# Moving two groups of matmuls in the block loop of a transformer layer: the gate's third pass and eight down products

## The chip, the cores and the metric

The kernel runs on one NeuronCore of one Trainium2 chip. TensorE (PE) multiplies into PSUM (8 banks of 128 x 512 float32 here); ScalarE (ACT), VectorE (DVE) and GpSimd (POOL) do the rest, of which GpSimd works on SBUF alone in this kernel; SyncE (SP) issues DMAs. Each engine takes its instructions in a fixed order and waits for others by semaphores. The metric is the device time of one execution in microseconds (us), as a median over runs.

## The reference: what is computed

8192 tokens (4 x 2048) of 256 features pass through one layer, post-norm, in float32:

```python
Q, K, V = x @ W_q.T, x @ W_k.T, x @ W_v.T
decay = sigmoid(log_decay[0])
mask = where(diff >= 0, decay ** diff, 0)        # 32 x 32, within a chunk of 32 tokens
S = einsum('bncd,bnkd->bnck', Qc, Kc) * mask     # scores, chunk by chunk
O = einsum('bnck,bnkd->bncd', S, Vc)
gate = sigmoid(x @ W_g.T)
attn = gate * O @ W_o.T + x
h = layernorm(x + attn)

g = h @ (w_gate / 127).T      # 768 hidden features, integer weights from -127 to 127
u = h @ (w_up / 127).T
out = layernorm(h + (silu(g) * u) @ (w_down / 127).T)
```

## The kernel before

The tokens are cut into 16 blocks of 512 (`TB`, `NB`). Everything is unrolled; a block's tensors lie either feature-major (features on partitions, 512 tokens along the row) or token-major (`NG` = 4 groups of 128 tokens).

**Parts.** To keep float32 accuracy on the fast matmul formats, operands are split in parts. An activation or weight of the attention becomes `hi`, `lo` and `gap` (`token_parts`, L464; `weight_parts`, L442): ScalarE makes `hi`, GpSimd makes `lo` = t - hi (L473), VectorE makes `gap` (L479, in a closure `gaps` that is called later). A product of two such operands is made by `three` (L526) in **three passes**: hi x hi and lo x lo go into a PSUM bank, ScalarE scales the bank in place (L533), then gap x gap is added (the third pass, in the closure `others`, L535) and `finish` reads the bank. Two banks are used per product. In the hidden layer `hT` and `u` are split in `hi` and an fp16 `lo` (L887/L888, L936/L937), the integer weights are stored in both types, and each product is hi x hi plus lo x lo.

**The loop.** Iteration `b` of L1141 (0 to 13) runs the hidden layer of block b, and beside it the attention of later blocks: `n = b + 2` is in its output projection, `m = b + 3` in its projections of y (the query and key matrices folded in one), value and gate. The hidden layer's 768 features come in six chunks of 128 (`ffn_up`, L900: fg and fu on PE, silu on ScalarE, the product u on VectorE, then the split: u_hi on ScalarE, u_lo on GpSimd). For b from 1 to 12 the order of PE's work, written out by hand, is:

1. chunks 0 and 1, the first two passes of y of block m, chunk 2, the third pass of y;
2. chunk 3, the scores `ps` of block m (L654; they read `yT`, the copy of y by VectorE, L558), the products with the values (L690) of block n, chunk 4;
3. the first two passes of the value (`split_v`) and of the gate (`split_gate`), the value's third pass (`v_rest`, L1199), chunk 5 (L1202);
4. the first two passes of the output projection (`split_out`, L1208), the **gate's third pass** (`g_rest`, L1211), whose results ScalarE turns into tanh (L550), and the output projection's third pass (`out_rest`, L1212), after which VectorE adds the residual (L820) and takes the mean and variance of the rows (L338, L339);
5. the **down product** of block b (`ffn_down`, L954): for b > 2 by `project_back_late` (L746), 24 products of high parts (six chunks of 128 hidden features, four token groups each), then 24 of low parts, into two banks.

The end of the iteration on the other engines, in program order: ScalarE casts the transposed h of block b + 1 (`split_h`, L887) right after the output projection's scaling and before the gate's tanh; then it makes x_hi of the block after m (`token_parts`, L1217), the two square roots of the layer norms (L347, between two table loads), and, in the next iteration, normalizes h (L426). GpSimd makes hT_lo (L888) and x_lo (L473). VectorE takes the moments, then `between` (L1223): the reciprocal, three small operations `minus`, `scale` and `shift` (L386 to L389), and the gaps of x; then the residual of the down product (L971) with its moments, and then u of the next block's chunk 0 (L931).

**What sets the order.** Nearly every instruction is pinned by `in_turn` (L115), which keeps program order on its engine; the splits of h on GpSimd and the DMAs are not pinned. PSUM banks are taken in turn from a pool of 8 (`bank`, L118), so that the bank of a new product is the one whose user came eight requests ago; the two banks of the down product are requested after the two of the output projection. DMAs go by SP's queue: per block one load of x, one of xT, one store of the output, and 16 small ones that move the 32 x 32 transposed pieces of h (L870).

Of the kernel before, what the change touches and what calls it, by code (L numbers as in the profile page):

```python
# [59 lines left out]
NG = TB // P  # L60
# [16 lines left out]
def kernel(  # L77
# [665 lines left out]
                    in_turn(product)  # L743
            finish(slice(h * per, (h + 1) * per), pb)

    def project_back_late(b, parts, ws, finish, name, between):  # L746


        per = TB // D
        banks = [bank(f"{name}_{b}_{h}") for h in range(NG // per)]  # L750
        hi, lo = (list(zip(part, w)) for part, w in zip(parts, ws))

        def product(g, part, w, first=False):
            in_turn(
                nc.tensor.matmul(  # L755
                    banks[g // per][:, g % per * D : (g % per + 1) * D],
                    lhsT=part[:, g * P : (g + 1) * P],
                    rhs=w,
                    start=first and g % per == 0,
                    stop=True,  # L760
                    skip_group_check=True,
                )
            )

        for i, term in enumerate(hi):
            for g in range(NG):
                product(g, *term, first=i == 0)
        for h in range(NG // per):
            for term in lo:
                for g in range(h * per, (h + 1) * per):  # L770
                    product(g, *term)
        between()
        for h, pb in enumerate(banks):
            finish(slice(h * per, (h + 1) * per), pb)

    def chunked(t):
        return [t[:, k, :] for k in range(t.shape[1])]
# [173 lines left out]
        hi, lo = (list(zip(part, w)) for part, w in zip(parts, ws))  # L951
        return hi[:-2] + lo[:-2], hi[-2:] + lo[-2:]

    def ffn_down(b, uT, h, between=None, chunkwise=False, amid=None):  # L954


        r = work.tile([P, NG, D], F32, tag="r2", name=f"r2_{b}")
        mv = no_moments(f"f{b}")
        made = None
        order = in_turn  # L960
        late_residuals = not chunkwise and b > 2

        def begin():
            nonlocal made
            if between is not None:
                made = between()

        def residual(gs, pb):

            order(  # L970
                nc.vector.scalar_tensor_tensor(  # L971
                    flat(r, gs), pb, SCALE**2 / U_UP * H_UP, flat(h, gs), ALU.mult, ALU.add
                )
            )
            moments(r, f"f{b}", range(gs.start, gs.stop), order, mv)
            if not late_residuals and gs.start == 0:
                begin()

        ws = [chunked(w) for w in fd]
        if chunkwise:  # L980
            per = TB // D
            banks = [bank(f"fdn_{b}_{k}") for k in range(NG // per)]
            for late, terms in enumerate(early_and_late(uT, ws)):
                if late and amid is not None:
                    made = amid()
                for k, pb in enumerate(banks):
                    for i, (part, w) in enumerate(terms):
                        for j in range(per):
                            g = k * per + j
                            product = nc.tensor.matmul(  # L990
                                pb[:, j * D : (j + 1) * D],
                                lhsT=part[:, g * P : (g + 1) * P],
                                rhs=w,
                                start=late + i + j == 0,
                                stop=True,
                                skip_group_check=True,
                            )
                            in_turn(product)
                    if late:
                        residual(slice(k * per, (k + 1) * per), pb)  # L1000
        else:
            if late_residuals:
                project_back_late(b, uT, ws, residual, "fdn", begin)
            else:
                project_back(b, uT, ws, residual, "fdn")
        return r, mv, made
# [134 lines left out]
    for b in range(NB - 2):  # L1141
        n = b + 2
        m = b + 3
        more = m < NB
        xns[n] = load_xn(n)
        if b and m + 1 < NB:
            xTs[m + 1] = load_xT(m + 1)
        hT = hTs.pop(b)
        uT = ([], []) if b else uT_0
        sT, v, sg = ahead  # L1150
        if not more:
            scales_next = iterated_scale_and_shift(mv_out, of_out, f"out_{b}")
        if b:
            normalize(hs[b + 1], *scales_h)
            up_now(b, hT, uT, 0)
        multiply = ffn_up(b, hT, uT, range(1, 2), held=True)
        if b:
            moving = move_h(b + 1, hs[b + 1])
        else:
            cast_fd(0, range(2, 3))  # L1160
            multiply()
            x_gaps()
            sT = attn_scores(n, yT)
            xTs[m + 1] = load_xT(m + 1)
        if more:
            yT, y_rest = split_y(m, x_parts)
        if b:
            multiply()
        if not more:
            goT = attn_values(n, sT, v, sg)  # L1170
        multiply = ffn_up(b, hT, uT, range(2, 3), held=True)
        if b > 1:
            normalize(r_before, *scales_out, range(NG // 2))
        multiply()
        if more:
            y_rest()
        if b == 0:
            normalize(hs[b + 1], *scales_h)
            moving = move_h(b + 1, hs[b + 1])
        if not more:  # L1180
            go_parts, go_gaps = token_parts(goT, f"go_{n}")
        multiply = ffn_up(b, hT, uT, range(3, 4), held=True)
        if b > 1:
            normalize(r_before, *scales_out, range(NG // 2, NG))
        multiply()
        if b > 1:
            store(b - 2, r_before)
        if more:
            sT_next = attn_scores(m, yT)
            goT = attn_values(n, sT, v, sg)  # L1190
            multiply = ffn_up(b, hT, uT, range(4, 5), held=True, low_first=True)
            go_parts, go_gaps = token_parts(goT, f"go_{n}")
            if b == 0:
                cast_fd(1, range(1))
            multiply()
            go_gaps()
            v_next, v_rest = split_v(m, x_parts)
            sg_next, g_rest = split_gate(m, x_parts)
            v_rest()  # L1199
            if b == 0:  # L1200
                cast_fd(1, range(1, 2))
            up_with_cast(b, hT, uT, 5, 1, range(2, 3))  # L1202
        else:
            up_now(b, hT, uT, 4)
            go_gaps()
        r_before = r_out
        if more:
            hs[n], out_rest = split_out(n, go_parts)  # L1208
            if b:
                hTs[b + 1] = split_h(b + 1, moving)  # L1210
            g_rest()  # L1211
            mv_h = out_rest()  # L1212
            if b == 0:
                hTs[b + 1] = split_h(b + 1, moving)
            ahead = sT_next, v_next, sg_next
            if m + 1 < NB:
                x_parts, x_gaps = token_parts(xTs[m + 1], f"x_{m + 1}")  # L1217
            std_h = root_in_turn(mv_h, of_h, f"h_{b}")
            if b:
                mv_before, std_before = mv_out, root_in_turn(mv_out, of_out, f"out_{b}")  # L1220
            back_to_silu()

            def between():  # L1223
                scales = scale_and_shift(
                    mv_h, std_h, of_h, f"h_{b}", nc.vector, in_turn
                )
                if m + 1 < NB:
                    x_gaps()
                return scales

            r_out, mv_out, scales_h = ffn_down(b, uT, hs.pop(b), between)
            if b:
                scales_out = scale_and_shift(mv_before, std_before, of_out, f"out_{b}")
        else:
            multiply = ffn_up(b, hT, uT, range(5, KH), held=True)
            hs[n], out_rest = split_out(n, go_parts)
            multiply()
            hTs[b + 1] = split_h(b + 1, moving)
            scales_out = scales_next
            normalize(r_before, *scales_out)  # L1240
            store(b - 1, r_before)

            def amid():
                return iterated_scale_and_shift(out_rest(), (HALF, 1.0), f"h_{n}")

            r_out, mv_out, scales_h = ffn_down(
                b, uT, hs.pop(b), chunkwise=True, amid=amid
            )
            scales_out = iterated_scale_and_shift(mv_out, of_out, f"out_{b + 1}")
# [361 lines left out]
```

## Time and profile before

| | before |
|---|---|
| median of 3 runs | 487.5 us (487.4 to 488.54) |
| the profiled execution, its own time | 486.83 us |
| span, first to last instruction | 485.2 us |
| granted TensorE clock, mean | 0.997 |
| period of one iteration, start of chunk 0 to the next (blocks 4 to 11) | about 29.2 us |
| busy in the stretch 192.29 to 221.50 us (block 5): PE, PEld, ACT, DVE, POOL | 29.21, 23.52, 22.95, 21.20, 16.72 us |
| mean duration: p_g third pass (128 x 512), p_o third pass (128 x 256), fdn high (128 x 256) | 393, 283, 281 ns |

The time is that of the whole execution on the device, the span that from the first to the last instruction of the program. PEld is the loading of the stationary operand into TensorE, which overlaps the matmuls. A matmul's duration contains the time that its last columns take through the array, so that consecutive matmuls overlap in the table: the pace is read from start to start (24 high down products from 216.12 to 218.95 us, so 0.118 us each, though one is listed with 281 ns). In a timeline each line gives the start, the length of the group, the engine, the line of the code, what is written from what, the shapes and the count; in brackets stands how long the engine was idle before it and what ended that.

### The profile page before, as it was taken

Reading aid. Unit: us, or ns where it says so; the run is one execution under the profiler, and the core shown is the slowest. Engines: PE = TensorE matmul, PEld = TensorE weight load, DVE = VectorE, ACT = ScalarE, POOL = GpSimd, SP = SyncE. Lnnn points to the kernel's source line nnn. Section 1 sums busy time; section 2 is a strip of 40 time slices with the busy share of each in tenths; the row PEclk is TensorE's granted clock in tenths of the full one; section 3 lists DMA queues with packets and bytes.
Section 4 is the critical chain, followed back from the end, with each engine's and each line's share of the span. In section 5 each row is a group of like instructions: output and inputs, shape, how many; then the busy total and the mean of one; then the engine's idle time right before and its main releaser. Section 6 shows DMA issues by size and latency. Waiting matters only on the chain.

```text
span 485.2 us, 12289 instructions
## 1 busy us (share of the span) xinstructions
PE 479.0 (99%) x4760; PEld 381.1 (79%) x4760; DVE 344.0 (71%) x795; ACT 371.3 (77%) x699; POOL 281.3 (58%) x285
## 2 busy tenths in 40 slices
PE   9999999999999999999999999999999999999995
PEld 5787787887868778797887968878697887868685
DVE  4687958687575976858777585975858777577656
ACT  4878697597887788687787877788687787776845
POOL 3835665555736565474555735566464655657764
PEclk9999999999999999999999999999999999999998
DMA  8720411211403114131321403113131211103002
GB/s 258 261 93 4 134 46 47 80 47 41 135 24 108 44 44 134 28 105 50 88 82 36 141 18 115 45 50 125 26 107 50 83 45 32 59 20 112 34 15 84
DMA packets 43323, 36.99 MB, mean 76 GB/s; under 512 B 4864, under 2 KB 39168, under 8 KB 43264
## 3 DMA queue, kind: packets, MB, share of 16 engines
q1 hardware_dynamic: 42144, 35.28, 23.8%
q10 hardware_dynamic: 1120, 0.92, 0.6%
q8 instruction: 38, 0.62, 0.6%
q14 instruction: 21, 0.17, 0.1%
HBM read 20.45 MB, written 8.39 MB: 59 GB/s over the span
## 4 chain that ended last, share of the span: by engine, by line
PE 99%; DVE 0%; ACT 0%; issue 0%
PE fg L911 18%; PE fu L911 18%; PE fdn L755 11%; PE p_o L514 9%; PE p_v L514 9%; PE p_y L492 9%; PE p_g L492 9%; PE po L690 4%; PE fdn L736 3%; PE ps L654 2%; PE fdn L990 2%; PE fdn L1353 1%; PE pg L578 1%; PE pv L620 1%; PE pa L799 1%; PE py L599 1%
## 5 line engine op out<-in xcount | busy, mean ns | idle before, releaser
L937 POOL TENSOR_TENSOR u_lo<-u,u_hi 128x512 f16<-128x512 f32 (+1 forms) x98 | 129.4, 1326 | 84.4 <-ACT u_hi L936 78.7
L931 DVE SCALAR_TENSOR_TENSOR u<-fu,s 128x512 f32<-128x512 f32 (+1 forms) x98 | 66.1, 675 | 72.5 <-ACT s L920 71.7
L936 ACT CAST u_hi<-u 128x512 fp32r<-128x512 f32 (+1 forms) x98 | 59.4, 606 | 45.7 <-DVE u L931 45.7
L920 ACT ACTIVATE s<-fg 128x512 f32<-128x512 f32 (+1 forms) x98 | 57.4, 585 | 41.5 <-PE fg L911 41.5
L911 PE MATMUL fg<-hT_hi,fg_hi 128*128 128x512 f32 (+1 forms) x196 | 72.8, 453 | 0.0
L911 PE MATMUL fu<-hT_hi,fu_hi 128*128 128x512 f32 (+1 forms) x196 | 60.3, 389 | 0.0
L911 PE MATMUL fg<-hT_lo,fg_lo 128*128 128x512 f16 (+1 forms) x196 | 58.2, 379 | 0.0
L911 PE MATMUL fu<-hT_lo,fu_lo 128*128 128x512 f16 (+1 forms) x196 | 57.4, 375 | 0.0
L473 POOL TENSOR_TENSOR go_lo<-goT,go_hi 128x512 fp32r<-128x512 f32 x30 | 44.6, 1510 | 18.2 <-ACT go_hi L472 18.2
L479 DVE SCALAR_TENSOR_TENSOR go_gap<-go_hi,goT 128x512 fp32r<-128x512 f32 x30 | 48.2, 1645 | 0.8 <-ACT go_hi L472 0.7
L473 POOL TENSOR_TENSOR x_lo<-xT,x_hi 128x512 fp32r<-128x512 f32 x30 | 37.7, 1277 | 14.1 <-ACT x_hi L472 14.1
L911 PEld LDWEIGHTS fg<-hT_hi,fg_hi 128*128 128x128 f32 x196 | 35.6, 190 | 10.3
L911 PEld LDWEIGHTS fu<-hT_hi,fu_hi 128*128 128x128 f32 x196 | 36.5, 188 | 8.1
L820 DVE TENSOR_TENSOR h<-p_o,x 128x512 f32<-128x512 f32 x30 | 19.3, 685 | 32.0 <-PE p_o L514 28.2
L888 POOL TENSOR_TENSOR hT_lo<-hT,hT_hi 128x512 f16<-128x512 f32 x28 | 35.7, 1296 | 4.0 <-ACT hT_hi L887 3.6
L911 PEld LDWEIGHTS <-fu_lo 128*128 128x128 f16 x196 | 19.2, 98 | 22.2
L388 POOL TENSOR_SCALAR minus_out<-rstd_out 128x4 f32<-128x4 f32 x12 | 2.6, 221 | 54.1 <-DVE rstd_out L386 54.1
L755 PE MATMUL fdn<-fd_hi,u_hi 128*128 128x256 f32 x240 | 29.9, 281 | 0.0
L755 PEld LDWEIGHTS fdn<-fd_hi,u_hi 128*128 128x128 f32 x240 | 29.0, 189 | 0.0
L911 PEld LDWEIGHTS <-fg_lo 128*128 128x128 f16 x196 | 13.1, 98 | 19.1 <-issue 12.9
L755 PE MATMUL fdn<-fd_lo,u_lo 128*128 128x256 f16 x240 | 27.9, 273 | 0.0
L426 ACT ACTIVATE h<-h,shift_h,scale_h 128x256 f32<-128x256 f32 x52 | 26.9, 587 | 0.7 <-DVE shift_h L389 0.7
(179 smaller groups left out, 1097.8 us busy)
## 6 DMA issues: line engine op xcount, KB each, us to landing
x<-in_x_dram SPq DMA_DIRECT2D x16, 512.0 KB, 3.8
xT<-in_xT_dram SPq DMA_DIRECT2D x15, 512.0 KB, 4.2
hT<-sq SPq DMA_DIRECT2D x224, 32.0 KB, 1.9
out_dram<-r SPq DMA_DIRECT2D x13, 512.0 KB, 3.2
out_dram<-r SPq DMA_DIRECT2D x7, 128.0 KB, 1.7
fg_int<-in_ffn_gT_dram SPq DMA_DIRECT2D x3, 256.0 KB, 7.4
fu_int<-in_ffn_uT_dram SPq DMA_DIRECT2D x3, 256.0 KB, 6.4
fd_int<-in_ffn_dT_dram SPq DMA_DIRECT2D x3, 256.0 KB, 5.5
```

What stands on the lines that cost most here:

```text
L426: nc.scalar.activation(r[:, g, :], r[:, g, :], AF.Identity, bias=shift[:, g : g + 1], scale=scale[:, g : g + 1],)
L473: in_turn(nc.gpsimd.tensor_tensor(lo[:, k, :], t[:, k, :], whole, ALU.subtract))
L479: nc.vector.scalar_tensor_tensor(gap[:, k, :], whole, -WHOLE, t[:, k, :], ALU.mult, ALU.add)
L492: nc.tensor.matmul(pb, lhsT=a[kind][:, k, i * P : (i + 1) * P], rhs=b[kind][:, k, :], start=kind + k == 0, stop=True, skip_group_check=True,)
L514: nc.tensor.matmul(pb[:, j * D : (j + 1) * D], lhsT=b[kind][:, k, g * P : (g + 1) * P], rhs=a[kind][:, k, :], start=kind + k + j == 0, sto ...
L755: nc.tensor.matmul(banks[g // per][:, g % per * D : (g % per + 1) * D], lhsT=part[:, g * P : (g + 1) * P], rhs=w, start=first and g % per ...
L888: nc.gpsimd.tensor_tensor(in_order[1], whole, in_order[0].bitcast(F32), ALU.subtract)
L911: product = nc.tensor.matmul(pb, lhsT=w[kind][:, dc, hc * P : (hc + 1) * P], rhs=hT[kind][:, dc, cols], start=(kind == kinds[0] and dc == ...
L920: in_turn(nc.scalar.activation(s, pg, AF.Silu, scale=SCALE / H_UP))
L931: nc.vector.scalar_tensor_tensor(u, pu, U_UP / H_UP, s, ALU.mult, ALU.mult)
L936: in_steady_turn(nc.scalar.copy(hi, u))
L937: in_steady_turn(nc.gpsimd.tensor_tensor(lo, u, hi.bitcast(F32), ALU.subtract))
```

## The change

In iterations with b > 2 that still prepare a later block (b = 3 to 12), two groups of matmuls take another place in PE's order:

- The gate's third pass (`g_rest`: 4 matmuls on PE and 2 tanh on ScalarE) is called directly after the value's third pass, ahead of chunk 5, and no longer between the output projection's first two passes and its third.
- `project_back_late` no longer runs the down product as a whole; it requests the banks and returns two functions, `high(chunks)` and `low()`. The first eight high products (chunks 0 and 1, four token groups each) are issued between the output projection's first two passes and its third; the other 16 and the 24 low ones follow the third pass as before, by `ffn_down`, which gets them in `begun`.

The small operations of `between`, the gaps and the residuals keep their order behind the low products. In iterations 0 to 2 and 13 and in the last two blocks the code does what it did.

```diff
-    def project_back_late(b, parts, ws, finish, name, between):
+    def project_back_late(b, parts, ws, name):
...
-        for i, term in enumerate(hi):
-            for g in range(NG):
-                product(g, *term, first=i == 0)
-        for h in range(NG // per):
-            for term in lo:
-                for g in range(h * per, (h + 1) * per):
-                    product(g, *term)
-        between()
-        for h, pb in enumerate(banks):
-            finish(slice(h * per, (h + 1) * per), pb)
+        def high(chunks):
+            for i in chunks:
+                for g in range(NG):
+                    product(g, *hi[i], first=i == 0)
+
+        def low():
+            for h in range(NG // per):
+                for term in lo:
+                    for g in range(h * per, (h + 1) * per):
+                        product(g, *term)
+            return [(slice(h * per, (h + 1) * per), pb) for h, pb in enumerate(banks)]
+
+        return high, low
...
-    def ffn_down(b, uT, h, between=None, chunkwise=False, amid=None):
+    def ffn_down(b, uT, h, between=None, chunkwise=False, amid=None, begun=None):
...
-        late_residuals = not chunkwise and b > 2
...
-            if not late_residuals and gs.start == 0:
+            if begun is None and gs.start == 0:
                 begin()
...
-            if late_residuals:
-                project_back_late(b, uT, ws, residual, "fdn", begin)
+            if begun is not None:
+                high, low, chunks = begun
+                high(chunks)
+                ready = low()
+                begin()
+                for gs, pb in ready:
+                    residual(gs, pb)
             else:
                 project_back(b, uT, ws, residual, "fdn")
...
             v_rest()
+            late = b > 2
+            if late:
+                g_rest()
...
             hs[n], out_rest = split_out(n, go_parts)
             if b:
                 hTs[b + 1] = split_h(b + 1, moving)
-            g_rest()
+            begun = None
+            if late:
+                high, low = project_back_late(b, uT, [chunked(w) for w in fd], "fdn")
+                high(range(2))
+                begun = high, low, range(2, KH)
+            else:
+                g_rest()
             mv_h = out_rest()
...
-            r_out, mv_out, scales_h = ffn_down(b, uT, hs.pop(b), between)
+            r_out, mv_out, scales_h = ffn_down(b, uT, hs.pop(b), between, begun=begun)
```

## The prediction

> **What bounds the kernel now.** I read the page first: busy shares and the chain that ended last.
>
> ```profile
> PE 479.0 (99%) x4760; PEld 381.1 (79%) x4760; DVE 344.0 (71%) x795; ACT 371.3 (77%) x699; POOL 281.3 (58%) x285
> ...
> PE 99%; DVE 0%; ACT 0%; issue 0%
> ```
>
> TensorE (PE) is hardly ever idle, so PE's order can only pay where PE waits, and a new wait costs its full length. Next the list of waits, for those of PE and of its weight loads (PEld):
>
> ```profile
> PEld ps L654 <- DVE yT L558: 4.4, 12, 0.4
> ```
>
> One wait recurs: the score products (ps) wait for VectorE's copy yT, 0.36 us of weight loading in each of 12 blocks. Third, the timelines of the engines in block 5, whose hidden layer starts at 192.29 and whose successor starts at 221.50 (period 29.21 us; the blocks from 163.08 to 425.94 all have 29.20 or 29.21). Columns are start and duration in us. PE:
>
> ```profile
> 209.69 1.09 PE L514 MATMUL p_v<-wv_gap,x_gap 128*128 128x256 f32 x8
> ...
> 211.96 0.62 PE L911 MATMUL fu<-hT_hi,fu_hi 128*128 128x512 f32 x2
> ...
> 214.26 1.08 PE L492 MATMUL p_g<-x_gap,wg_gap 128*128 128x512 f32 x4
> 215.17 1.10 PE L514 MATMUL p_o<-wo_gap,go_gap 128*128 128x256 f32 x8
> 216.12 2.99 PE L755 MATMUL fdn<-fd_hi,u_hi 128*128 128x256 f32 x24
> ...
> 231.07 0.63 PE L911 MATMUL fu<-hT_hi,fu_hi 128*128 128x512 f32 x2
> 231.63 0.76 PE L654 MATMUL ps<-yT,xT 128*32 128x32 f32 x64
> ```
>
> From start to start the gate's third pass takes 0.91, the output projection's third pass 0.95, 24 high down products 2.83 (0.118 each). The last fu before ps takes 0.56 where others take 0.46: PE loses 0.10 us per block at ps and nothing that I can see elsewhere. So at the place of the change there is no wait to remove. What matters is who feeds yT. ScalarE, GpSimd, VectorE, in order of time:
>
> ```profile
> 212.16 0.60 ACT L920 ACTIVATE s<-fg 128x512 f32<-128x512 f32 x1 [0.67 <-PE fg L911]
> 213.57 0.62 ACT L936 CAST u_hi<-u 128x512 fp32r<-128x512 f32 x1 [0.81 <-DVE u L931]
> 214.09 1.06 ACT L533 ACTIVATE p_o<-p_o 128x512 f32<-128x512 f32 x2
> 215.08 1.13 ACT L887 CAST hT_hi<-hT 128x512 fp32r<-128x512 f32 x2
> ...
> 215.77 2.56 POOL L888 TENSOR_TENSOR hT_lo<-hT,hT_hi 128x512 f16<-128x512 f32 x2 [0.21 <-ACT hT_hi L887]
> 218.28 2.51 POOL L473 TENSOR_TENSOR x_lo<-xT,x_hi 128x512 fp32r<-128x512 f32 x2
> ...
> 220.09 0.73 DVE L388 TENSOR_SCALAR minus_h<-rstd_h 128x4 f32<-128x4 f32 x1
> 225.79 0.66 DVE L931 SCALAR_TENSOR_TENSOR u<-fu,s 128x512 f32<-128x512 f32 x1
> ...
> 226.48 0.62 ACT L936 CAST u_hi<-u 128x512 fp32r<-128x512 f32 x1 [2.48 <-DVE u L931]
> 227.50 1.07 ACT L533 ACTIVATE p_y<-p_y 128x512 f32<-128x512 f32 x2
> 229.00 0.61 ACT L920 ACTIVATE s<-fg 128x512 f32<-128x512 f32 x1
> ...
> 229.69 0.69 DVE L931 SCALAR_TENSOR_TENSOR u<-fu,s 128x512 f32<-128x512 f32 x1 [1.31 <-ACT s L920]
> 230.30 1.28 DVE L558 COPY yT<-p_y 128x512 f32<-128x512 f32 x2
> ...
> 424.37 0.17 DVE L388 TENSOR_SCALAR minus_h<-rstd_h 128x4 f32<-128x4 f32 x1
> ```
>
> Read this as one chain with no slack. Chunk 5's silu starts 0.04 us after its PE product ends (211.30 + 0.82 = 212.12). u, u_hi, the two scalings of p_o and the hT_hi copies follow back to back on ScalarE; hT_lo starts when the first hT_hi is done; x_lo follows hT_lo on GpSimd without a gap and ends at 220.79. VectorE's minus_h, 128x4 elements, takes 0.73 us and ends at 220.82, 0.03 after x_lo. In all nine blocks 3 to 11 it takes 0.72 or 0.73 and ends about 0.03 after x_lo; in block 12, where no x_lo runs, it takes 0.17. So it is held until x_lo is done. VectorE then works without a gap to u of the next block's chunk 0 (225.79), which ScalarE has awaited for 2.48 us; from 226.48 ScalarE has no gap to silu 2, which releases u 2, which releases yT, which ends at 231.58; ps starts at 231.63. From ps to the next chunk 5 PE is dense. That loop sets the period: PE from ps to chunk 5, the side engines from chunk 5 to ps.
>
> **The change part by part.** No instruction is added or removed: PE's work per block stays 29.1 plus the 0.10 lost. No DMA is issued by a moved step, and neither SP's nor GpSimd's queue gets another order.
>
> First, the gate's third pass (4 products, 0.91 us) goes ahead of chunk 5. PE reaches chunk 5 0.91 later counted from ps. It needs ScalarE's second scaling of p_g, which here ran 209.89 to 210.47; the pass would start at 210.62 and need that bank at 211.08: free, with 0.6 to spare. Its two tanh (1.09 us on ScalarE, after hT_hi at 216.11 now) move ahead of chunk 5's silu, past u_hi, the p_o scalings and hT_hi. They would run from the end of the v copies (211.48) to 212.5, and the silu can then start only at 212.16 + 0.91 = 213.07: hidden in ScalarE's idle time there, at a price of nothing; without that cover 1.09. Taking the tanh from behind hT_hi brings x_hi 1.09 nearer to hT_hi, but x_lo queues behind hT_lo, not for x_hi (ready at about 217.7, used at 218.28), so nothing is gained.
>
> Everything from chunk 5's silu to the end of x_lo then comes 0.91 later: x_lo ends at 220.79 + 0.91 = 221.70, minus_h at 221.73.
>
> Second, eight high products (8 x 0.118 = 0.94) go between the output projection's passes. They cover the wait for ScalarE's scaling of p_o as the gate's pass did (0.94 for 0.91), so the third pass finds its banks ready as before. Their inputs, u_hi of chunks 0 and 1, are many us old; the banks come in the same order as before (p_o, then fdn) and were last read by the v copies, done at 211.48. Without that cover: ScalarE's two scalings, up to 1.06 per block. But the third pass ends 0.94 later from ps, and h, its moments (now 215.91 to 219.34) and rstd_h with it. ScalarE's rstd_h now starts at 219.55, at the end of a table load and not of the moments; so it comes at about 220.35, 0.80 later, and minus_h would be ready at 220.89, still ahead of 221.70. This second shift hides behind the first; alone it would reach past today's 220.79 by (220.89 + 0.17) - 220.82 = 0.24.
>
> So the side chain starts 0.91 later and is not shorter: u 0, the p_y scalings, silu 2 and yT all come 0.91 later, and ps starts at about 232.54. PE would have been ready at 231.53. The value's y third pass sees it first: its bank 0 is scaled at 227.50 + 0.58 + 0.91 = 228.99 where its weight load now starts at 228.59, 0.40 late; chunk 3 behind it then ends near 232.0, still before ps. That 0.40 is therefore part of the 0.91, unless stalls add. Queued behind ps on PE are the value products, chunk 4 and all else: the block is late by 0.91.
>
> Blocks 3 to 11 have such an end (x_lo and the score products of the next block): nine times. Block 12 has no x_lo; its rstd_h waits for the moments and its successor has no y pass and no scores: 0 to 0.3, taken as 0. PE's changes of size and type between passes (0.95 against 0.91 for the same work) bound the reorder itself by 0.03 x 10 = 0.3 either way, taken as 0. Sum: 9 x 0.91 = **8.2 us**. Against the profiled execution, 486.83 (span 485.2): 495.0. The runs' median, 487.5, is 0.67 above it: **495.7**.
>
> The Trainium skill, "SBUF — State Buffer", section "Who interferes with whom", says that VectorE and GpSimd share a pair of ports held for a whole instruction, that tensor_scalar on VectorE can take it, and that the one that comes second is blocked until the other is done. The minus_h rows agree (0.73 beside x_lo, 0.17 without). By that rule the held minus_h gives the 495.7; were the 0.73 something else, the shift would be the 0.80 of the moments and the time 494.7. The rule speaks against the change, as what delays GpSimd delays VectorE's smallest instruction.
>
> **The rivals.** (1) minus_h is not tied to x_lo and only the late moments count: 9 x 0.80 = 7.2, 494.7. Against it: nine equal ends at 0.03 after x_lo. (2) The stalls add: the y pass's 0.40 is not regained before ps: 9 x 1.31 = 11.8, 499.3. Against it: PE's 1.78 us of chunk 3 (229.75 to 231.53) fit before 232.54. (3) Not slower: the tanh out of ScalarE's way shortens the chain, because x_hi and not GpSimd's queue is what x_lo awaits. ScalarE's chain after hT_hi would then lose 1.09 and gain 0.91, and PE would lose at ps none of today's 0.10: 9 x 0.10 = 0.9 less, 486.6. It decides from x_hi being the later one, i.e. if x_lo started within 0.1 of x_hi's end; it starts 0.6 after it and right at hT_lo's end. (4) The chain has slack that the trace hides, and the move changes nothing: 487.5. For it, PE's busy shares; against it, the rows above.
>
> **How the numbers follow.** Forecast 0.74, rival 1 0.08, rival 2 0.08, rival 3 0.03, rival 4 0.07. The time is the forecast's, 495.7. The range goes down to rival 1 less the 0.3 of the reorder and about 1 for the spread of runs (487.4 to 488.54), 493.4, and up to 495.7 + 0.3 + 0.3 + 1.1 = 497.4, a partial rival 2; about 0.18 lies outside. A change under 0.3%, 1.5 us, can't be told from none: slower 0.91, same 0.07, faster 0.02 (rival 3 beyond its own 0.9, or a gain not seen here).
>
> **What would show it.** In the profile after: period of blocks 4 to 12 about 30.1; PE late at ps and at the y pass, with yT as the releaser; minus_h ending just after x_lo, and x_lo ending 0.9 later after ps than now; the tanh between the v copies and chunk 5's silu; no wait of PE at the moved gate pass or at the third pass of p_o. It is wrong if ps doesn't wait longer than now, if x_lo doesn't move with chunk 5, or if ScalarE is late at p_o.

## The result, and the profile after

The changed kernel takes 494.65 us (median of 4 runs, 494.31 to 495.19) against 487.45 us before (median of 4, 487.39 to 488.54): ratio 1.0147, 95% interval 1.0135 to 1.016, or 7.2 us more. The profiled execution took 494.79 us, its span 493.2. That is inside the range and 1.05 us under the predicted 495.7; the loss was forecast as 8.2 and is 7.2.

The page of the changed kernel, busy shares and the chain that ended last:

```profile
PE 482.4 (98%) x4760; PEld 377.8 (77%) x4760; DVE 347.1 (70%) x795; ACT 370.4 (75%) x699; POOL 280.9 (57%) x285
...
PE 62%; DVE 23%; ACT 7%; issue 3%; SPq 2%; DMA 1%; DVEq 0%; ACTq 0%
```

TensorE's busy share fell by one point only, but the chain is another one: VectorE and ScalarE now hold 30% of it, where they held nothing. The list of waits (us in total, times, longest) names the places:

```profile
PEld p_y L492 <- ACT p_y L533: 8.4, 20, 0.7
PEld ps L654 <- DVE yT L558: 8.2, 22, 0.4
...
PE ps L654 <- DVE yT L558: 2.7, 10, 0.3
...
PE p_y L492 <- ACT p_y L533: 1.9, 9, 0.2
```

In the list of before, PE itself waited once (1.0 us, at the program's start). Now it waits nine times for the scaling of p_y, once in each of the blocks 4 to 12, and ten times at the scores, in the same blocks and once near the program's start. The waits of the weight loads are longer than what PE loses, since part of each would have been looking ahead; the loss itself is read from start to start. The timeline of PE at the end of block 6 and in block 7 (start and duration in us, then engine, line, operation):

```profile
235.48 1.16 PE L690 MATMUL po<-sT,v 64*64 64x64 f32 x64
...
242.96 1.08 PE L492 MATMUL p_g<-x_gap,wg_gap 128*128 128x512 f32 x4
...
245.22 0.62 PE L914 MATMUL fu<-hT_hi,fu_hi 128*128 128x512 f32 x2
247.52 1.07 PE L755 MATMUL fdn<-fd_hi,u_hi 128*128 128x256 f32 x8
248.43 1.07 PE L514 MATMUL p_o<-wo_gap,go_gap 128*128 128x256 f32 x8
...
251.15 2.79 PE L755 MATMUL fdn<-fd_lo,u_lo 128*128 128x256 f16 x24
...
260.59 0.59 PE L914 MATMUL fu<-hT_lo,fu_lo 128*128 128x512 f16 x2
261.39 1.22 PE L492 MATMUL p_y<-x_gap,m_gap 128*128 128x512 f32 x4 [0.21 <-ACT p_y L533]
262.45 0.61 PE L914 MATMUL fg<-hT_lo,fg_lo 128*128 128x512 f16 x2
263.78 0.63 PE L914 MATMUL fu<-hT_hi,fu_hi 128*128 128x512 f32 x2
264.33 0.27 PE L654 MATMUL ps<-yT,xT 128*32 128x32 f32 x8
264.88 0.70 PE L654 MATMUL ps<-yT,xT 128*32 128x32 f32 x56 [0.28 <-DVE yT L558]
265.51 1.16 PE L690 MATMUL po<-sT,v 64*64 64x64 f32 x64
```

The lines of PE before that these are set against, beside those shown ahead of the result:

```profile
203.12 1.16 PE L690 MATMUL po<-sT,v 64*64 64x64 f32 x64
...
218.95 2.79 PE L755 MATMUL fdn<-fd_lo,u_lo 128*128 128x256 f16 x24
...
228.38 0.59 PE L911 MATMUL fu<-hT_lo,fu_lo 128*128 128x512 f16 x2
...
229.75 0.60 PE L911 MATMUL fg<-hT_lo,fg_lo 128*128 128x512 f16 x2
...
232.32 1.16 PE L690 MATMUL po<-sT,v 64*64 64x64 f32 x64
```

From the last low product before the y pass to the end of that pass (260.59 to 262.45) PE takes 1.86 us, where it took 1.37 (228.38 to 229.75): 0.49 lost. The scores take 1.18 (264.33 to 265.51) where they took 0.69 (231.63 to 232.32): 0.49 lost, and their first eight records now start on the first half of yT and the other 56 wait for the second. Against that, the output projection's third pass and the 24 high down products together take 3.63 (247.52 to 251.15) instead of 3.78 (215.17 to 218.95), 0.15 gained. 0.49 + 0.49 - 0.15 = 0.83, and the period is 30.03 instead of 29.20 or 29.21. The side engines in the same stretch:

```profile
243.72 1.10 ACT L550 ACTIVATE sg<-p_g 128x512 f32<-128x512 f32 x2
245.42 0.60 ACT L923 ACTIVATE s<-fg 128x512 f32<-128x512 f32 x1 [0.59 <-PE fg L914]
248.35 1.13 ACT L890 CAST hT_hi<-hT 128x512 fp32r<-128x512 f32 x2
252.62 0.30 ACT L347 ACTIVATE rstd_h<-mv_a,eps 128x4 f32<-128x4 f32 x1 [0.78 <-DVE mv_a L339]
...
249.04 2.55 POOL L891 TENSOR_TENSOR hT_lo<-hT,hT_hi 128x512 f16<-128x512 f32 x2 [0.21 <-ACT hT_hi L890]
251.53 2.51 POOL L473 TENSOR_TENSOR x_lo<-xT,x_hi 128x512 fp32r<-128x512 f32 x2
...
253.16 0.91 DVE L388 TENSOR_SCALAR minus_h<-rstd_h 128x4 f32<-128x4 f32 x1
259.04 0.66 DVE L934 SCALAR_TENSOR_TENSOR u<-fu,s 128x512 f32<-128x512 f32 x1
...
260.75 1.07 ACT L533 ACTIVATE p_y<-p_y 128x512 f32<-128x512 f32 x2
...
263.55 1.28 DVE L558 COPY yT<-p_y 128x512 f32<-128x512 f32 x2
```

Follow the loop once round, in four distances. From the start of chunk 5's last products to the end of x_lo: 8.82 us (245.22 to 254.04), before 8.83 (211.96 to 220.79). From there to the end of yT: 10.79 (to 264.83), before 10.79 (to 231.58). From there to the start of the value products: 0.68 (to 265.51), before 0.74 (to 232.32). From the start of the value products to chunk 5's last products, all on PE: 9.74 (235.48 to 245.22), before 8.84 (203.12 to 211.96). The four add up to the periods, 30.03 and 29.20. The side chain is as long as it was, to 0.01 us; PE reaches its start 0.90 later. minus_h again ends 0.03 after x_lo (254.07), now with 0.91 us instead of 0.73.

### The profile page after: what moved, and what is told of

The parts are those of the page before. It is cut to its first block, busy times and chain, and to the rows that moved or that the text cites. A ratio compares the mean times of both kernels' runs of the same rounds, so it can differ in the third digit from the quotient of the medians.

```text
span 493.2 us, 12290 instructions
## 1 busy us (share of the span) xinstructions
PE 482.4 (98%) x4760; PEld 377.8 (77%) x4760; DVE 347.1 (70%) x795; ACT 370.4 (75%) x699; POOL 280.9 (57%) x285
## 4 chain that ended last, share of the span: by engine, by line
PE 62%; DVE 23%; ACT 7%; issue 3%; SPq 2%; DMA 1%; DVEq 0%; ACTq 0%
PE fg L914 10%; PE fu L914 10%; PE p_v L514 8%; PE p_g L492 8%; PE p_o L514 7%; PE po L690 3%; DVE u L934 3%; DVE st_f L338 3%; PE fdn L755 3%; PE p_y L492 3%; DVE x_gap L479 3%; ACT s L923 2%; DVE yT L558 2%; DVE st_a L338 2%; DVE r L973 2%
```

## The experiments

The theory: the gate's third pass makes chunk 5 late, chunk 5 makes x_lo late, x_lo holds VectorE's minus_h, and from there the chain runs to the scores. The main rival: the eight down products make the output projection's third pass late, and its moments set the loss; its price, 9 x 0.80 = 7.2 us, is just what was measured, so the result alone cannot tell the two apart. Each ratio is to the kernel before, run on the same chip.

**The gate alone.**

```diff
                 high, low = project_back_late(b, uT, [chunked(w) for w in fd], "fdn")
-                high(range(2))
-                begun = high, low, range(2, KH)
+                begun = high, low, range(KH)
```

> The gate's third pass ahead of chunk 5 as in the changed kernel, all 24 high down products behind the output projection's third pass as before. Theory (chunk 5 late, so x_lo on GpSimd late, so VectorE's minus_h held): the same as the changed kernel, 494.0 to 495.2 us, minus_h still ending about 0.03 us after x_lo, period about 30.03; TensorE's uncovered wait for the scaling of p_o (up to 0.45 us a block) lies where it has 0.8 us a block to lose anyway. Rival (the late third pass of the output projection sets the loss, by its moments): it comes 0.94 less 0.45 us earlier, so 9 x 0.5 = 4.4 us less than the changed kernel, about 490.2.

Measured: 495.36 us, ratio 1.0161 (1.0144 to 1.0178), the whole loss, and 0.16 us over the expected range. In its timelines (PE, GpSimd, VectorE):

```profile
247.52 1.22 PE L514 MATMUL p_o<-wo_gap,go_gap 128*128 128x256 f32 x8 [0.31 <-ACT p_o L533]
...
251.07 2.50 POOL L473 TENSOR_TENSOR x_lo<-xT,x_hi 128x512 fp32r<-128x512 f32 x2
...
252.37 1.23 DVE L388 TENSOR_SCALAR minus_h<-rstd_h 128x4 f32<-128x4 f32 x1
```

The moments are ready earlier, so minus_h is issued earlier relative to x_lo and is held for 1.23 us instead of 0.91; it ends at 253.60, 0.03 after x_lo (253.57). PE's new wait for p_o costs next to nothing per block, as expected (period 30.04 against 30.03): it falls where PE is to wait later anyway. In block 12, which has no x_lo behind it, it is paid: from the value products of block 12 to those of block 13 this kernel takes 22.64 us, the changed one 22.03. That is about the 0.7 us by which this kernel's median lies above the changed one's.

**The down products alone.**

```diff
             v_rest()
             late = b > 2
-            if late:
-                g_rest()
...
             if late:
+                g_rest()
                 high, low = project_back_late(b, uT, [chunked(w) for w in fd], "fdn")
                 high(range(2))
```

> Eight high down products ahead of the output projection's third pass, the gate's third pass in its old place before them. Theory: x_lo comes as in the kernel before, minus_h is ready 0.24 us after today's end, of which about 0.08 is slack before the score products: 9 x 0.16 = 1.4 us, 488.9 us, minus_h no longer held (0.2 us and less). Rival (moments): 0.80 us a block, 9 x 0.80 = 7.2, about 494.7.

Measured: 488.75 us, ratio 1.002 (1.001 to 1.003), 1.1 us more than the 487.64 before. GpSimd, VectorE, and PE at the scores:

```profile
249.18 2.51 POOL L473 TENSOR_TENSOR x_lo<-xT,x_hi 128x512 fp32r<-128x512 f32 x2
...
251.76 0.17 DVE L388 TENSOR_SCALAR minus_h<-rstd_h 128x4 f32<-128x4 f32 x1
...
262.53 0.91 PE L654 MATMUL ps<-yT,xT 128*32 128x32 f32 x64
263.37 1.16 PE L690 MATMUL po<-sT,v 64*64 64x64 f32 x64
```

x_lo ends at 251.69, minus_h starts after that and takes 0.17. The period of the blocks is 29.33, 0.13 over the kernel before (0.16 expected), and the scores take 0.84 instead of 0.69 (262.53 to 263.37). So the rival's path exists, but on its own it is worth about a seventh of the loss.

**The changed kernel, first residual first.**

```diff
                 ready = low()
-                begin()
                 for gs, pb in ready:
                     residual(gs, pb)
+                    if gs.start == 0:
+                        begin()
```

> The changed kernel, with the small operations and x's gaps on VectorE behind the first residual of the down product and its moments, not ahead of them. Theory: VectorE works while x_lo runs, and its 0.91 us of minus_h shrinks to 0.17; u of chunk 0 comes 0.74 us earlier: 9 x 0.74 = 6.7 us less, about 488.0 us. Rival (no hold; minus_h is long for a reason of its own, or the moments alone set u): same work in another order, 494.0 to 495.2, minus_h again about 0.9 us.

Measured: 486.92 us, ratio 0.9981 (0.9972 to 0.9991): the loss is gone, and a little more (1.1 us under the expected 488.0). GpSimd, VectorE, and PE at the scores:

```profile
278.42 2.51 POOL L473 TENSOR_TENSOR x_lo<-xT,x_hi 128x512 fp32r<-128x512 f32 x2
...
279.56 0.69 DVE L973 SCALAR_TENSOR_TENSOR r<-fdn,h 128x512 f32<-128x512 f32 x1
281.55 0.17 DVE L388 TENSOR_SCALAR minus_h<-rstd_h 128x4 f32<-128x4 f32 x1
...
290.72 0.76 PE L654 MATMUL ps<-yT,xT 128*32 128x32 f32 x64
```

VectorE works on the residual while x_lo runs (to 280.93), and minus_h comes after it. The 64 score records run without a break again, and the period is 29.07, 0.14 less than before.

**The changed kernel, hT_hi ahead of chunk 5's u_hi.**

```diff
-            up_with_cast(b, hT, uT, 5, 1, range(2, 3))
+            if late:
+                multiply = ffn_up(b, hT, uT, range(5, KH), held=True)
+                hTs[b + 1] = split_h(b + 1, moving)
+                multiply()
+            else:
+                up_with_cast(b, hT, uT, 5, 1, range(2, 3))
...
-            if b:
+            if b and not late:
                 hTs[b + 1] = split_h(b + 1, moving)
```

> The changed kernel, with the hT_hi casts on ScalarE (and so hT_lo and x_lo on GpSimd) moved ahead of chunk 5's u_hi, from behind the scalings of p_o. Theory: x_lo ends about 1.1 us earlier than in the changed kernel, minus_h is not held (0.2 us), and what remains is the 0.24 us of the late moments less 0.08 of slack: 9 x 0.16 = 1.4 us, 488.9 us. Rival (moments alone): no change, 494.0 to 495.2.

Measured: 487.92 us, ratio 1.001 (1.0 to 1.0019), 1 us less than expected; the period is 29.29. Its GpSimd, VectorE, and PE at the scores:

```profile
244.62 2.54 POOL L891 TENSOR_TENSOR hT_lo<-hT,hT_hi 128x512 f16<-128x512 f32 x2 [2.54 <-ACT hT_hi L890]
247.12 1.31 POOL L940 TENSOR_TENSOR u_lo<-u,u_hi 128x512 f16<-128x512 f32 x1
248.37 2.53 POOL L473 TENSOR_TENSOR x_lo<-xT,x_hi 128x512 fp32r<-128x512 f32 x2
...
251.17 0.17 DVE L388 TENSOR_SCALAR minus_h<-rstd_h 128x4 f32<-128x4 f32 x1
...
261.86 0.99 PE L654 MATMUL ps<-yT,xT 128*32 128x32 f32 x64
262.78 1.16 PE L690 MATMUL po<-sT,v 64*64 64x64 f32 x64
```

x_lo is done at 250.90, ahead of minus_h, though chunk 5 comes late and the order of VectorE is that of the changed kernel. The period lies 0.08 over the kernel before, but 0.22 over the third experiment, which has the same order on PE (29.07). The 0.22 is found at the scores, which take 0.92 (261.86 to 262.78) where the third experiment's take 0.69. It is put down to the late moments, as in the second experiment; it was not taken apart further.

**The kernel before, first residual first.** (`between()` taken out of `project_back_late`, and called in `residual` after the first group pair.)

```diff
-            if not late_residuals and gs.start == 0:
+            if gs.start == 0:
                 begin()
```

> The kernel before, with the small operations and x's gaps behind the first residual of the down product. Theory (TensorE has no real wait in the kernel before, so a shorter side chain buys nothing): minus_h 0.17 us, period 29.2 us, time as before, 487.2 to 488.0 us. Rival (the order of the residual is itself what put the third experiment under the kernel before): about 486.9 us, 0.7 less.

**The second experiment, first residual first** (the two diffs together).

> The second experiment (gate's third pass in its old place, eight down products ahead of the output projection's third pass) with the first residual first. Theory: TensorE waits nowhere, and its own pace with the gate's pass directly ahead of the 128x256 products (0.118 us each for the high down products) sets the period, 29.2 us: 487.2 to 488.0 us. Rival (the pace comes from splitting the 24 high products in 8 and 16): period 29.07 us as in the third experiment, 486.9 us.

Measured: 488.16 us, ratio 1.0013 (1.0004 to 1.0022), for the former, and 487.62 us, ratio 1.0003 (0.9994 to 1.0012), for the latter; before 487.33. Both rivals fall. The former is 0.2 us over its range, though its period is the expected 29.21. In the profiled runs its span is 1.0 us longer than before, and none of that lies in blocks 3 to 12. Some 0.53 us of it stand at the program's start, ahead of all that was edited: the first value products start at 25.35 instead of 24.82. In the ten profiled runs this start lies between 24.82 and 26.14, the latter in the third experiment; whether it belongs to the kernel or to the run stays open. Some 0.44 us stand in block 13, which takes 20.73 us from its chunk 0 to that of block 14, before 20.29. The four kernels with the first residual first all have this (20.71 to 20.74), and in each PE waits there for GpSimd's go_lo (0.16 us at 439.69 in the former), as in none of the others. So that order, which keeps minus_h clear of x_lo in blocks 3 to 11, goes with some 0.4 us more at the end of the loop, where no x_lo runs beside minus_h. The high down products of the former, then of the latter, on PE:

```profile
245.88 2.99 PE L755 MATMUL fdn<-fd_hi,u_hi 128*128 128x256 f32 x24
```

```profile
244.71 1.10 PE L755 MATMUL fdn<-fd_hi,u_hi 128*128 128x256 f32 x8
246.60 2.05 PE L755 MATMUL fdn<-fd_hi,u_hi 128*128 128x256 f32 x16
```

From start to start they take 2.83 us in the former and 0.94 + 1.89 = 2.83 in the latter, with the period at 29.21 in both. In the third experiment, with the gate's pass gone from there, they take 0.91 + 1.82 = 2.73, and in the first, with all 24 in one piece, 2.72. The output projection's third pass beside them takes 0.95 in the latter and 0.91 in the third. So the 0.14 us a block (0.10 and 0.04) that the third experiment lies under the kernel before come from where the gate's pass stands, not from splitting the high products and not from the residual.

**The third experiment from block 1 on** (`late = b > 0`).

> The third experiment with the changed order in blocks 1 and 2 too. Theory: two more blocks of TensorE's shorter pace, 0.14 us each: 0.3 us less than the third experiment, about 486.6 us. Rival (blocks 1 and 2 differ and have no slack for the later chunk 5): up to 0.9 us a block more, 488.7 us.

Measured: 486.67 us, ratio 0.9982 (0.9973 to 0.9991). The period of blocks 1 and 2 is 29.07 as in the others, so there was slack there; the gain over the third experiment, 0.25 us between runs on two chips, can't be told from none.

**minus_h and scale_h written with a stride.**

```diff
+        if eng is nc.vector:
+            minus, scale = (
+                small.tile([P, NG, 2], F32, tag=f"{tag}_2", name=f"{tag}_2_{name}")[:, :, 0]
+                for tag in ("minus", "scale")
+            )
```

> The changed kernel with minus_h and scale_h written to every second element of a row, the values the same. Theory: the small VectorE operations wait for the end of x_lo whichever of them comes first; if the stride frees minus_h (0.17 us), shift_h, which reads two tensors, is held in its place, and the time stays at 494.0 to 495.2 us. Rival (minus_h alone is slow, by its form): it falls to 0.2 us with no other taking its place, 9 x 0.7 us less, 488.3 us.

Measured: 494.35 us in its one execution. VectorE:

```profile
252.58 0.91 DVE L393 TENSOR_SCALAR minus_h<-rstd_h 128x4 f32<-128x4 f32 x1
253.41 0.15 DVE L393 TENSOR_SCALAR scale_h<-rstd_h 128x4 f32<-128x4 f32 x1
```

The stride frees nothing, and the hold stays on the first instruction. The rival falls; which of minus_h and shift_h would be held if the first were free, this run can't say.

## Why the prediction was right, and where its size was off

**No wait to remove at the old place.** Right: with the changed order and the side chain out of the way (third experiment) the period falls by 0.14 us only, and that is pace, not a wait.

**The chain from chunk 5 by way of x_lo.** Right, and shown: chunk 5 late without the down products gives the loss (first), the down products without a late chunk 5 give 1.1 us of it (second), and taking x_lo out of minus_h's way takes the loss away, on VectorE's side (third) as on GpSimd's (fourth). The rival of the late moments, priced at 494.7, met the measured 494.65 almost to the digit for a wrong reason; only the parts done alone told it from the forecast.

**The tanh ahead of chunk 5's silu cost nothing.** Right: they ran from 243.72 to 244.82, and ScalarE was still idle for 0.59 us before the silu.

**Eight down products cover the scaling of p_o.** Right: PE goes into the third pass at 248.43 without a wait; without that cover it waits there (first experiment).

**"PE loses 0.10 us per block at ps".** This is the step that failed, and with it the "no slack" behind the term 9 x 0.91. The 0.56 us of the last product before the scores is not a wait for yT. It is 0.56 in the kernel before at block 3 too, where yT was done 0.42 us ahead of the scores (PE, then VectorE):

```profile
143.46 0.63 PE L911 MATMUL fu<-hT_hi,fu_hi 128*128 128x512 f32 x2
144.02 0.77 PE L654 MATMUL ps<-yT,xT 128*32 128x32 f32 x64
```

```profile
142.32 1.28 DVE L558 COPY yT<-p_y 128x512 f32<-128x512 f32 x2
```

So PE in the kernel before did not wait at the scores, and the chain had a little slack there. From the end of yT to the start of the value products it had 0.74 us, and where PE does wait for yT it is 0.67 or 0.68 (the changed kernel, and the second and fourth experiments, in each of these blocks), as four of the scores' 32 products can run on the first half of yT. PE's shift, 0.90, less this 0.06 is 0.84 by these rows and 0.83 by the periods; nine times 0.83 is 7.5, the figure of the traces (value products of block 12 at 415.64 against 407.56, less 0.63 by which the changed run was late before block 3: 7.45). The medians differ by 7.2.

**The y pass.** It was said to be 0.40 late, all of it part of the scores' delay. It loses 0.49, and the scores another 0.49 on top; less the 0.15 gained among the down products, the two make up the 0.83 by which the period grew.

**PE's changes of size "within 0.3, taken as 0".** The gain of 0.15 a block is real but was worth nothing here, since it lies between chunk 5 and the scores, where PE had become the one that waits. From block 12 on nothing was lost (from block 12's value products to the end of the span 77.56 us, before 77.64).

## What to carry to other kernels

An engine that is busy 99% of the time can still sit in a loop with a side chain of the same length: measure the chain around the loop, link by link, before moving work into the part of the loop that the chain waits for. Here a delay of what starts the chain was paid nearly in full (0.83 of 0.91 us a block), and a delay of 0.94 off the chain cost 0.13. When a tiny instruction has a long duration, look at what another engine finishes in the same moment, and give the first engine other work until then: that alone took the whole loss of 7 us away here. Look at the end of the loop too, where nothing holds the tiny instruction and the new order only delays it.

## What the runs showed of the hardware

VectorE's minus_h, a tensor_scalar on 128x4 elements, takes 0.17 us by itself; issued while GpSimd's x_lo runs, it lasts until the running x_lo is done: 0.73 us in the kernel before, 0.91 in the changed one, 1.23 with the gate alone, each time ending 0.03 us after x_lo. Not every instruction is held: the reciprocal just ahead of it, also 128x4, takes 0.18 us beside x_lo (from 219.88 in the kernel before) and 0.18 without it (from 250.96 in the fourth experiment). A residual with one operand in PSUM isn't held either (0.69 us beside x_lo in the third experiment, 0.68 without it in the fourth). The hold of minus_h and the free residual agree with the Trainium skill's "SBUF — State Buffer", section "Who interferes with whom", which names tensor_scalar among the operations that can take the ports shared with GpSimd, and leaves free an instruction with at most one input in SBUF outside the two-port modes. That a stride on the output doesn't free minus_h agrees with "VectorE: DVE Perf Modes", section "Mode 2×_2P", which asks for SBUF operands and an even outermost dimension, but for no unit step.

The same 24 products of 128x256 take 2.83 us with the gate's four products of 128x512 just ahead of that stretch, and 2.72 or 2.73 without. The granted clock was 1.00 in both kinds of stretch (214.20 to 221.50 before, 246.60 to 253.70 in the changed kernel, whose products also take 2.72), so it is not the clock. What of the array or of its weight loads makes that difference stays open; no run took it apart.
